# Gated linear attention: the last two out projections from seven block products, and a new place for VectorE's rank comparisons

## The chip, the cores and the metric

The kernel runs on one core of a Trainium2 chip. The metric is the device time of one execution in microseconds (us). Three executions of the kernel before the change took 910.1, 910.58 and 911.43 us; their median, 910.58 us, is the time that the changed kernel is compared with. All arithmetic is in float32; in the first feed-forward stage, alone, operands are split in two rounded parts.

## What is computed

The reference is a stack of four blocks on x of 2 x 1024 rows of 512 numbers, each followed by a layernorm. The change lies at the end of the third block and the beginning of the fourth. Cut to that:

```python
# third block: gated linear attention, o from a chunked scan
go = o @ Wog.T + x @ Wig.T
on = o * rsqrt(mean(o * o) + EPS) * g_norm_w
x  = layernorm(x + (on * (go * sigmoid(go))) @ Wo.T)
# fourth block: half of each batch's rows, by their score, go through a feed-forward
scores = x @ router_weight + router_bias
top, indices = top_k(scores, 512)                  # of 1024, for each batch
h = gelu(x[indices] @ w1 + b1)                     # 512 -> 2048
x[indices] += (h @ w2 + b2) * sigmoid(top)
x = layernorm(x)
```

## The kernel before, in words

The 2048 rows are worked on as four blocks of 512 rows, blk 0 to 3; batch 0 is blocks 0 and 1, batch 1 is blocks 2 and 3. Matrix products go to TensorE (PE), which writes to eight accumulation banks. They are picked from two rings of four, `mm_bank` and `acc_bank`; the fourth block alternates between the rings (`either_bank`, line 1528). VectorE (DVE) does the adds, the row statistics and the comparisons, ScalarE (ACT) the copies out of banks and the activations, GpSimd (POOL) a few sums, the powers and the gathers by index, and SyncE (SP) issues the other transfers.

Each engine runs its own queue in order. Where two queues meet, a semaphore makes one wait. The framework's scheduler sets each queue's order from the program, and `tc.issue_after(ins)` holds the instructions inside it back until `ins` has been placed: it is how the kernel's author moves work in a queue.

**Seven products for eight.** A product of matrices cut in 2 x 2 blocks needs eight block products. Most products of this kernel use seven, with sums of blocks made ahead on VectorE. In `finish_by_seven` (line 1375) the left factor is u (the gated rows, stored transposed in the tile uT), the right factor is W1o. `sums_of_W1o` (line 1358) makes four tiles T1 to T4 from W1o once; `sums_of_u` (line 1365) makes S1, S2 and A11 - A21 for each block of rows, three instructions. A product is four matmuls of 128 x 256, its result is added to x by two VectorE instructions (line 1393), and bank `grow` is added to by four products in turn, so that the next of them can only start once VectorE has read the last. `finish` (line 1410) does the same job with the plain sixteen matmuls of 128 x 512 and one add for each 128 rows (line 1423). Before the change blocks 0 and 1 use `finish_by_seven`, and blocks 2 and 3 use `finish`.

**The order around it.** The loop at line 1776 runs over blk. `attend(blk)` makes o of this block (tiles op, line 1257 and 1269), `gate(blk)` is a generator with the seven products of its gate (tiles go, line 864), between which the loop puts the out projection of block blk - 1. After it `scored_rows(blk - 1)` (line 1427) takes row statistics, the power on GpSimd, the layernorm and four scores. In blk 2, `route(0, ...)` ranks batch 0: eight transposes of the scores (tile rp, line 1458), then for each of eight columns two comparisons and one test for equals, each with a running sum (tiles cmp, lines 1467, 1470, 1473), then the ranks as an index (line 1480) and eight gathers on GpSimd (line 1483) that write the picked rows to HBM. `fetch(b)` (line 1506) reads them back and transposes them (tiles xs, xsTp).

**The fourth block.** `hidden(b, xs, h, beside)` (line 1532) computes h for one batch in four groups, g = 0 to 3, of seven products (tiles hp, line 1546); after each come VectorE's adds, lines 1558 to 1564 and 1571. Its sums of w1 are made by `sums_of_w1` (line 1848), its sums of x by `sums_of_x` (line 1516). The dictionary `beside` says what is placed between: `first_ranks` after the sixth product of group 0 holds the eight transposes of batch 1's scores and the first three columns of its ranking, the entry 0 has the sums of w1 for group 2 and then the other six steps of the ranking, and `next_rows`, after the sixth product of group 3, fetches batch 1's picked rows. `unpicked(blk)` (line 1498) normalizes a block once more and writes it to the output; block 0 is done in the loop's last round. Tiles of x, `x_room(i)`, and W1oT, the room of T1 to T4, are used again for sums of x, for h and for `kept`.

Of the kernel before, what the change touches and what calls it, by code (L numbers as in the profile page):

```python
# [21 lines left out]
P = 128  # L22
B, T, C = 2, 1024, 512
NB = 4
# [49 lines left out]
def body(ctx: ExitStack, tc: tile.TileContext, a: dict, out: bass.AP):  # L74
# [666 lines left out]
    class Gates:  # L741
# [10 lines left out]
            nc.scalar.copy(self.k4, lg[:, :, :, 32:])  # L752
            self.lq, self.lk = self.q4, self.k4

        def whole(self, lp):
            lg = lp.rearrange("p (i g d) -> p g i d", g=2, d=64)
            self.lq, self.lk = lg[:, :, :, :32], lg[:, :, :, 32:]
            self.k_exp()
            self.k_inverse()
            self.k_log()  # L760
            self.q_below()
            self.q_exp()
            self.q_share()
# [601 lines left out]
    def sums_of_u():  # L1365
# [6 lines left out]
        ins = nc.vector.tensor_sub(A21, A11, A21).ins  # L1372
        return (A11, A12, A21, A22), (S1, S2), ins

    def finish_by_seven(blk, u, w):

        (A11, A12, A21, A22), (S1, S2) = u
        (B11, B21, B22), (T1, T2, T3, T4) = w

        def product(ps, a, b, first, s, o):  # L1380

            with tc.issue_after(last_3[0]) if last_3[0] else contextlib.nullcontext():
                for r in range(2):
                    for m in range(2):
                        ins = nc.tensor.matmul(  # L1385
                            ps[:, 256 * r : 256 * r + 256], a[:, m, r * P : (r + 1) * P], b[:, m],
                            start=first and r == 0 and m == 0, stop=m == 1, skip_group_check=True,
                        ).ins
            last_3[0] = ins
            for r in range(2):  # L1390
                i = 2 * s + r
                x = x_t[blk][:, i, 256 * o : 256 * o + 256]
                nc.vector.scalar_tensor_tensor(
                    x, ps[:, 256 * r : 256 * r + 256], inv[blk][:, i : i + 1], x, ALU.mult, ALU.add
                )

        grow, p2, side = acc_bank("grow3"), mm_bank("P2"), mm_bank("P7")
        product(grow, A11, B11, True, 0, 0)
        product(p2, A12, B21, True, 0, 0)
        nc.vector.tensor_sub(A12, A12, S2)  # L1400
        yield
        product(grow, S2, T2, False, 1, 0)
        product(side, A21, T3, True, 1, 1)
        yield
        product(grow, S1, T1, False, 1, 1)
        product(side, A22, T4, False, 1, 0)
        product(grow, A12, B22, False, 0, 1)
        yield

    def finish(blk):  # L1410


        ao = [acc_bank("ao3") for _ in range(4)]
        steps = [(i, n) for i in range(4) for n in range(4)]
        if blk == NB - 1:
            steps = [(0, 0), (0, 1), (1, 0), (1, 1), (0, 2), (0, 3), (1, 2), (1, 3)] + steps[8:]
        for i, n in steps:
            k = (0, 2, 1, 3)[n]
            last_3[0] = nc.tensor.matmul(ao[i], uT[blk][:, k, i * P : (i + 1) * P], W1o[:, k], start=n == 0, stop=n == 3).ins  # L1419
        mv = sp.tile([P, 4, 2], F32, tag="mv", name="mv")  # L1420
        for i in range(4):
            x = x_t[blk][:, i]
            nc.vector.scalar_tensor_tensor(x, ao[i], inv[blk][:, i : i + 1], x, ALU.mult, ALU.add)
            row_stats(mv[:, i], x)
        return scored_rows(blk, mv)

    def scored_rows(blk, mv=None):

# [103 lines left out]
    def hidden(b, xs, h, beside):  # L1532

        (B11, B21, B22), (T1, T2, T3, T4) = xs

        def gelu(f):
            x = h[f // 4][:, f % 4]
            nc.scalar.activation(x, x, AF.Gelu_apprx_tanh, bias=b1[:, f : f + 1])

        def product(w, g, x):  # L1540

            ps = either_bank("hp")
            with tc.issue_after(last_hp[0]) if last_hp[0] else contextlib.nullcontext():
                for j in range(2):
                    for k in range(2):
                        ins = nc.tensor.matmul(  # L1546
                            ps[:, 256 * j : 256 * j + 256], pair_of(w, g)[:, k, j], x[:, k], start=k == 0, stop=k == 1
                        ).ins
            last_hp[0] = ins
            return ps.rearrange("p (j t) -> p j t", j=2)  # L1550

        for g in range(4):

            c = h[g].rearrange("p (j e) (s t) -> p j e s t", e=2, s=2)
            c11, c12, c21, c22 = (c[:, :, e, s] for e in range(2) for s in range(2))
            nc.scalar.copy(c11, product(wA11, g, B11))
            p2 = product(wA12, g, B21)
            nc.vector.tensor_add(c12, c11, product(wS2, g, T2))
            nc.vector.tensor_add(c11, c11, p2)
            nc.vector.tensor_add(c21, c12, product(wS3, g, T3))  # L1560
            p5 = product(wS1, g, T1)
            nc.vector.tensor_add(c22, c21, p5)
            nc.vector.tensor_add(c12, c12, p5)
            nc.vector.tensor_add(c12, c12, product(wS4, g, B22))
            if ("last", g) in beside:

                with tc.issue_after(last_hp[0]):
                    last_hp[0] = beside["last", g]()
            for j in range(2):
                gelu(4 * g + 2 * j)  # L1570
            ins = nc.vector.tensor_sub(c21, c21, product(wA22, g, T4)).ins
            for j in range(2):
                gelu(4 * g + 2 * j + 1)
            if g in beside:
                with tc.issue_after(ins):
                    beside[g]()
# [5 lines left out]
    def finish_ffn(w2, h):  # L1582
# [56 lines left out]
                add(ps, x, w, r)  # L1639
            return ps  # L1640

        kept = x_room(0, "kept")

        def steps(b):

# [128 lines left out]
    with tc.issue_after(scored):  # L1774
        next(ending)
    for blk in range(NB):
        if blk == 1 or blk == 2:
            *sums, summed = sums_of_u()
            if blk == 1:
                with tc.issue_after(summed):  # L1780
                    W1o_sums = sums_of_W1o()
        if blk == 2:
            new_front(3, gates)
        if blk == 1:
# [4 lines left out]
        if blk == 1:  # L1789
            with tc.issue_after(last_op[0]):  # L1790
                lp = turned_logits(lT)
            last_3[0] = last_turned[0]
            gates = Gates([wk.tile([P, 8, 32], F32, tag=n, name=n) for n in ("q3", "k3", "l3")])
            gates.whole(lp)
        if blk:
            o_sum(blk)
            gating = gate(blk)
            if blk < 3:
                finishing = finish_by_seven(blk - 1, sums, W1o_sums)
                for n in range(2):  # L1800
                    next(finishing)
                    next(gating)
                    if blk == 1 and n == 1:
                        with tc.issue_after(last_3[0]):
                            last_3[0] = gates.decayed(kd_room, jk.tile([P, 8, 32], F32, tag="junk", name="e3"))
                next(finishing)
                scored = scored_rows(blk - 1)
            else:
                scored = finish(blk - 1)
                for _ in range(2):  # L1810
                    next(gating)
        next(gating)
        if blk == 2:
            ranking = route(0, xT_tile("row"))
# [4 lines left out]
        if blk == 0:  # L1819
            o_sum(0)  # L1820
            nc.sync.dma_start(out=rw, in_=a["rw"].to_broadcast([P, C]))
            nc.sync.dma_start(out=b2, in_=a["b2"].to_broadcast([P, C]))
        other_sums(blk)
        if blk == 0:
            with tc.issue_after(scored_next):
                next(ending, None)
# [3 lines left out]
        for n, done in enumerate(gating):  # L1830
            if n == blk == 0:
                rms(0, sum2)
            if n == 2 and blk == 0:
                with tc.issue_after(last_3[0]):
                    last_3[0] = turn(3)
            if n == 1 and blk < 3:
                with tc.issue_after(done):
                    x_sum(blk + 1)
            if blk == 2:
                with tc.issue_after(done):  # L1840
                    for _ in range((3, 2, 2, 3)[n]):
                        next(ranking)
    wS1, wS2, wS4 = (spare[i][:, :, :512].rearrange("p (k h) (j f) -> p k h j f", h=2, f=P) for i in range(3))

    def pair_of(w, g):
# [10 lines left out]
                ins = nc.vector.tensor_tensor(pair_of(dst, g), pair_of(x, g), pair_of(y, g), op).ins  # L1856
        return ins

    sums_of_w1((0,))
    _, xs = fetch(0)  # L1860
    xs = sums_of_x(xs, W1oT)
    finish(3)
    sums_of_w1((1,))
    s3.close()
    wk = ctx.enter_context(tc.tile_pool(name="s4", bufs=2))
    h = [[*(wk.tile([P, 4, 512], F32, name=f"h0{g}", bufs=1) for g in range(3)), o_room]]
# [2 lines left out]
        nc.sync.dma_start(out=w2[g], in_=a["w2"][512 * g : 512 * (g + 1), :].rearrange("(f p) d -> p f d", p=P))  # L1869
    room = xT_tile("row")  # L1870
    ranking = route(1, room)

    def x_room(i, name):
        return xpool.tile([P, 4, ROW], F32, tag=f"x{i}", name=name)[:, :, :C]

    later = []

# [6 lines left out]
        return last_turned[0]  # L1884

    def next_sums():
        later[1] = sums_of_x(later[1], x_room(0, "xsums"))

    def first_ranks():
        rank_some(4)  # L1890
        return last_turned[0]

    hidden(0, xs, h[0], {("last", 0): first_ranks, ("last", 3): next_rows, 0: lambda: (sums_of_w1((2,)), rank_some(6)), 1: lambda: sums_of_w1((3,)), 3: next_sums})
    h.append([xT_tile("h10"), W1oT, later[0], x_room(1, "h13")])
    hidden(1, later[1], h[1], {g: lambda g=g: unpicked(g + 1) for g in range(3)})
    finish_ffn(w2, h)

# [51 lines left out]
```

## Time and profile before

| what | us |
|---|---|
| median of three executions | 910.58 |
| the profiled execution | 911.5 |
| its span, from its first instruction to its last | 909.7 |
| PE busy in the span | 891.9 |
| DVE busy in the span | 677.5 |
| ACT busy | 382.2 |
| POOL busy | 261.7 |

The profiled execution is 1.8 us longer than its span and 0.9 us above the median. PE is busy for 98% of the span, but a busy engine is only an average: in the stage of the change, between 640 and 760 us, PE still waits for others at some places. The granted clock of TensorE is 1.00 throughout that stage. A row of the timeline has the start and the length of a group of instructions on one engine, the line in the code, the operation, the tile written and the tile read, the shapes and a count; a matmul of float32 counts as two. In brackets stands how long the engine was idle before the group, and who released it.

### The profile page before, as it was taken

The page shows a single profiled execution, that of the slowest core. Times are in us where ns is not written, and L with a number is a line of the kernel's source. Part 1 is how long each engine was busy: PE and PEld are TensorE (multiplying, and loading weights), DVE is VectorE, ACT ScalarE, POOL GpSimd, SP SyncE. Part 2 cuts the span into 40 slices and gives each one's busy share as a digit, 9 for nine tenths or more (in the row PEclk, how much of TensorE's full clock was granted, in tenths as well). Part 3 has the DMA queues.
Part 4 walks back from the last instruction along what each step waited for, and adds up shares of the span by engine and source line. Part 5 has one row for each costly group of instructions (what it writes and reads, how often), then busy time and mean ns, then how long its engine had stood idle before and what let it go on. Part 6 is the DMA issues. An engine that isn't in the chain of part 4 may idle for free.

```text
span 909.7 us, 10988 instructions
## 1 busy us (share of the span) xinstructions
PE 891.9 (98%) x4037; PEld 698.8 (77%) x4037; DVE 677.5 (74%) x1304; ACT 382.2 (42%) x652; POOL 261.7 (29%) x229
## 2 busy tenths in 40 slices
PE   8999999999999999999999999999999999999996
PEld 5668786687688888888877677788676888888886
DVE  2569995589777787787769875857977976898535
ACT  2345343463467777877867534231201223120000
POOL 1120075200574357455654302020250030000112
PEclk9999999999999999999999999999999999999999
DMA  9632221200400000001001500000024220230001
GB/s 321 215 100 79 66 72 47 70 1 0 123 6 1 0 1 13 35 1 46 1 1 47 209 1 1 1 0 1 1 94 139 93 85 10 99 134 0 12 36 47
DMA packets 26135, 50.17 MB, mean 55 GB/s; under 512 B 4798, under 2 KB 5482, under 8 KB 25569
## 3 DMA queue, kind: packets, MB, share of 16 engines
q1 hardware_dynamic: 23441, 44.34, 14.5%
q0 software_dynamic: 1920, 4.22, 1.2%
q10 hardware_dynamic: 720, 0.92, 0.4%
q8 instruction: 32, 0.52, 0.3%
q14 instruction: 22, 0.18, 0.1%
HBM read 41.03 MB, written 10.54 MB: 57 GB/s over the span
## 4 chain that ended last, share of the span: by engine, by line
PE 81%; DVE 13%; ACT 2%; issue 2%; DMA 1%; POOL 0%; POOLq 0%; SPq 0%; DVEq 0%
PE yp L1632 10%; PE yp L896 9%; PE gatep L896 9%; PE hp L1546 9%; PE upp L896 9%; PE go L864 7%; PE xk L412 6%; PE grow L361 4%; PE P L361 3%; PE ao L559 2%; PE ao L1419 2%; PE grow L1385 1%; PE kp L585 1%; DVE cmp L1470 1%; PE op L1257 1%
## 5 line engine op out<-in xcount | busy, mean ns | idle before, releaser
L955 DVE TENSOR_TENSOR yp<-yp,ratio 128x512 f32<-128x512 f32 x160 | 103.3, 693 | 15.1 <-PE yp L896 15.0
L210 POOL TENSOR_TENSOR rs<-rs,table 128x4 f32<-128x4 f32 (+1 forms) x19 | 17.2, 904 | 293.8 <-DVE rs L209 293.6
L921 ACT ACTIVATE gatep<-gatep,scale 128x512 f32<-128x512 f32 x132 | 85.1, 656 | 34.9 <-PE gatep L896 32.2
L896 PE MATMUL yp<-wdn,hhi 128*128 128x512 f32 x176 | 71.7, 408 | 0.0
L896 PE MATMUL gatep<-x1Th,wgu 128*128 128x512 f32 x176 | 70.2, 399 | 0.0
L896 PE MATMUL yp<-wdn,hlo 128*128 128x512 f32 x176 | 69.8, 397 | 0.2 <-POOL hlo L930 0.2
L896 PE MATMUL gatep<-x1Tl,wgu 128*128 128x512 f32 x176 | 69.2, 393 | 0.3 <-DVE x1Tl L241 0.3
L896 PE MATMUL upp<-x1Tl,wgu 128*128 128x512 f32 x176 | 69.0, 392 | 0.0
L896 PE MATMUL upp<-x1Th,wgu 128*128 128x512 f32 x176 | 68.8, 391 | 0.0
L921 ACT ACTIVATE upp<-upp,scale 128x512 f32<-128x512 f32 x88 | 57.8, 662 | 11.1 <-PE upp L896 7.2
L930 POOL TENSOR_TENSOR hlo<-whole,hhi 128x512 fp32r<-128x512 f32 x43 | 55.6, 1292 | 3.5
L929 POOL CAST hhi<-whole 128x512 fp32r<-128x512 f32 x43 | 26.3, 612 | 99.8 <-DVE whole L927 89.6
L927 DVE SCALAR_TENSOR_TENSOR whole<-upp,scale,silu 128x512 f32<-128x512 f32 x43 | 32.3, 751 | 25.2 <-PE upp L896 19.0
L864 PE MATMUL go<-spare,spare 128*128 128x256 f32 x192 | 44.0, 381 | 0.0
L217 DVE BATCH_NORM_STATS2 st<-x 128x6 f32<-128x512 f32 x64 | 42.4, 679 | 0.4
L412 PE MATMUL xk<-pair,x 128*128 128x512 f32 x96 | 42.7, 592 | 0.0
L864 PEld LDWEIGHTS go<-spare,spare 128*128 128x128 f32 x192 | 36.0, 190 | 5.8 <-issue 1.2
L1279 POOL TENSOR_TENSOR sum<-sum,sq 128x512 f32<-128x512 f32 x12 | 18.2, 1520 | 77.1 <-issue 67.5
L896 PEld LDWEIGHTS gatep<-x1Th,wgu 128*128 128x128 f32 x176 | 33.1, 188 | 9.2 <-ACT gatep L921 1.3
L896 PEld LDWEIGHTS yp<-wdn,hhi 128*128 128x128 f32 x176 | 33.1, 188 | 8.8 <-DVE yp L955 1.1
L923 DVE TENSOR_SCALAR upp<-upp,scale 128x512 f32<-128x512 f32 x44 | 33.0, 753 | 9.1 <-PE upp L896 8.0
L896 PEld LDWEIGHTS gatep<-x1Tl,wgu 128*128 128x128 f32 x176 | 33.1, 188 | 8.0 <-DVE x1Tl L241 0.6
(468 smaller groups left out, 2109.5 us busy)
## 6 DMA issues: line engine op xcount, KB each, us to landing
pk<-in_gu SPq DMA_DIRECT2D x16, 352.0 KB, 3.6
x<-in_x SPq DMA_DIRECT2D x4, 1024.0 KB, 14.6
w<-in_w SPq DMA_DIRECT2D x1, 4096.0 KB, 12.3
xs<-picked SPq DMA_DIRECT2D x4, 1024.0 KB, 5.2
out<-x SPq DMA_DIRECT2D x4, 1024.0 KB, 4.2
w<-in_w SPq DMA_DIRECT2D x4, 1024.0 KB, 6.5
x0T<-in_xT SPq DMA_DIRECT2D x3, 1024.0 KB, 7.9
pk<-in_dn SPq DMA_DIRECT2D x11, 256.0 KB, 3.2
```

The source lines that it names most:

```text
L217: nc.vector.bn_stats(st, x)
L361: ins = nc.tensor.matmul(ps[:, 256 * r : 256 * r + 256], a[:, k, r * P : (r + 1) * P], b[:, k], start=first and r == 0 and k == 0, stop=k ...
L412: ins = nc.tensor.matmul(acc_of[b][c], x_t[blk][:, i, c * P : (c + 1) * P], pairs_of["k", blk][i // 2][:, i % 2], start=blk % 2 == 0 and i ...
L864: ins = nc.tensor.matmul(ps[:, 256 * m : 256 * m + 256], w[:, k, m], b[:, k, 256 * half : 256 * half + 256], start=first and m == 0 and k ...
L896: nc.tensor.matmul(ps, w, x, start=start and n == 0, stop=stop and n == 1, skip_group_check=True)
L921: nc.scalar.activation(ps, ps, AF.Copy, scale=s)
L923: nc.vector.tensor_scalar(ps, ps, s, None, ALU.mult)
L927: nc.vector.scalar_tensor_tensor(self.whole, ps, s, self.silu, ALU.mult, ALU.mult)
L930: nc.gpsimd.tensor_sub(lo, self.whole, hi.bitcast(F32))
L955: nc.vector.tensor_tensor(self.y[:, i] if g == NI - 1 else ps, ps, ratio[:, g], ALU.mult)
L1546: ins = nc.tensor.matmul(ps[:, 256 * j : 256 * j + 256], pair_of(w, g)[:, k, j], x[:, k], start=k == 0, stop=k == 1).ins
L1632: nc.tensor.matmul(ps[:, 256 * r : 256 * r + 256], x(r, j), w(j), start=j == 0, stop=j == NJ - 1)
```

## The change

1. Blocks 2 and 3 use `finish_by_seven` too, and `finish` is gone. `sums_of_u` runs in each round, and once more after the loop.
2. In round 1, the gates' later steps (`rest`) are placed after the adds of the first product (`first_add`); in each round `other_sums` are placed after those of the third (`second_add`).
3. The ranking of batch 0 had its ten steps all in round 2, as 3, 2, 2, 3 between the gate's parts. It has 1, 3, 1, 0 there, two after round 3's sums of u and three after `first_add`.
4. The sums of w1 for groups 0 and 1 are placed after the add of the last gate's fifth product (`gate_sums_end`).
5. In `hidden(0, ...)` the last six steps of batch 1's ranking are placed one at a time between the adds of group 1 and no longer ahead of them.
6. Rooms: the sums of x for batch 0 go into the room of block 0's x, which `unpicked(0)` writes out, as W1oT is still in use; those of batch 1 into W1oT.

```diff
-        def whole(self, lp):
+        def begin(self, lp):
             ...
             self.k_exp()
+
+        def rest(self):
             self.k_inverse()
...
+                ins_of[0] = nc.vector.scalar_tensor_tensor(
                     x, ps[:, 256 * r : 256 * r + 256], inv[blk][:, i : i + 1], x, ALU.mult, ALU.add
+                ).ins
+            return ins_of[0]
...
+        first_add[blk] = product(grow, A11, B11, True, 0, 0)
...
+        second_add[blk] = product(grow, S2, T2, False, 1, 0)
...
+            def add(*x):
+                nonlocal added
+                added += 1
+                ins = nc.vector.tensor_add(*x).ins
+                if (g, added) in beside:
+                    with tc.issue_after(ins):
+                        beside[g, added]()
...
-        kept = x_room(0, "kept")
+        kept = W1oT
...
-        if blk == 1 or blk == 2:
+        if blk:
             *sums, summed = sums_of_u()
-            if blk == 1:
-                with tc.issue_after(summed):
+            with tc.issue_after(summed):
+                if blk == 1:
                     W1o_sums = sums_of_W1o()
+                if blk == 3:
+                    for _ in range(2):
+                        next(ranking)
...
+            finishing = finish_by_seven(blk - 1, sums, W1o_sums)
+            for n in range(2):
                 next(finishing)
+                if blk == 1 and n == 0:
+                    with tc.issue_after(first_add[0]):
+                        gates.rest()
+                if blk == 3 and n == 0:
+                    with tc.issue_after(first_add[2]):
+                        for _ in range(3):
+                            next(ranking)
+                next(gating)
...
-        other_sums(blk)
+        with tc.issue_after(second_add[blk - 1]) if blk else contextlib.nullcontext():
+            other_sums(blk)
...
-                    for _ in range((3, 2, 2, 3)[n]):
+                    for _ in range((1, 3, 1, 0)[n]):
                         next(ranking)
+            if blk == 3 and n == 1:
+                gate_sums_end = done
...
-    sums_of_w1((0,))
+    with tc.issue_after(gate_sums_end):
+        sums_of_w1((0,))
+    *sums, _ = sums_of_u()
     _, xs = fetch(0)
-    xs = sums_of_x(xs, W1oT)
-    finish(3)
-    sums_of_w1((1,))
+    xs = sums_of_x(xs, x_room(0, "xsums0"))
+    for _ in finish_by_seven(3, sums, W1o_sums):
+        pass
+    scored_rows(3)
+    with tc.issue_after(gate_sums_end):
+        sums_of_w1((1,))
...
-    hidden(0, xs, h[0], {("last", 0): first_ranks, ("last", 3): next_rows, 0: lambda: (sums_of_w1((2,)), rank_some(6)), 1: lambda: sums_of_w1((3,)), 3: next_sums})
-    h.append([xT_tile("h10"), W1oT, later[0], x_room(1, "h13")])
+    one_rank = lambda: rank_some(1)
+    hidden(0, xs, h[0], {
+        ("last", 0): first_ranks, ("last", 3): next_rows, 0: lambda: (sums_of_w1((2,)), one_rank()), 1: lambda: sums_of_w1((3,)),
+        (1, 2): one_rank, (1, 3): one_rank, (1, 5): one_rank, (1, 6): lambda: rank_some(2), 3: next_sums,
+    })
+    h.append([xT_tile("h10"), x_room(0, "h11"), later[0], x_room(1, "h13")])
```

More of the change, by code (lines that the diff above doesn't have):

```diff
@@ L1373, in sums_of_u @@
         return (A11, A12, A21, A22), (S1, S2), ins
+    first_add, second_add = {}, {}
     def finish_by_seven(blk, u, w):
@@ L1392, in product @@
                 x = x_t[blk][:, i, 256 * o : 256 * o + 256]
-                nc.vector.scalar_tensor_tensor(
+                ins_of[0] = nc.vector.scalar_tensor_tensor(
                     x, ps[:, 256 * r : 256 * r + 256], inv[blk][:, i : i + 1], x, ALU.mult, ALU.add
-                )
+                ).ins
+            return ins_of[0]
+        ins_of = [None]
         grow, p2, side = acc_bank("grow3"), mm_bank("P2"), mm_bank("P7")
-        product(grow, A11, B11, True, 0, 0)
+        first_add[blk] = product(grow, A11, B11, True, 0, 0)
         product(p2, A12, B21, True, 0, 0)
@@ L1401, in finish_by_seven @@
         yield
-        product(grow, S2, T2, False, 1, 0)
+        second_add[blk] = product(grow, S2, T2, False, 1, 0)
         product(side, A21, T3, True, 1, 1)
@@ L1408, in finish_by_seven @@
         yield
[L1410 to L1425, printed above, removed]
     def scored_rows(blk, mv=None):
@@ L1556, in hidden @@
             nc.scalar.copy(c11, product(wA11, g, B11))
+            added = 0
+            def add(*x):
[5 more added lines that the diff above has]
+                        beside[g, added]()
             p2 = product(wA12, g, B21)
-            nc.vector.tensor_add(c12, c11, product(wS2, g, T2))
-            nc.vector.tensor_add(c11, c11, p2)
-            nc.vector.tensor_add(c21, c12, product(wS3, g, T3))
+            add(c12, c11, product(wS2, g, T2))
+            add(c11, c11, p2)
+            add(c21, c12, product(wS3, g, T3))
             p5 = product(wS1, g, T1)
-            nc.vector.tensor_add(c22, c21, p5)
-            nc.vector.tensor_add(c12, c12, p5)
-            nc.vector.tensor_add(c12, c12, product(wS4, g, B22))
+            add(c22, c21, p5)
+            add(c12, c12, p5)
+            add(c12, c12, product(wS4, g, B22))
             if ("last", g) in beside:
@@ L1793, in body @@
             gates = Gates([wk.tile([P, 8, 32], F32, tag=n, name=n) for n in ("q3", "k3", "l3")])
-            gates.whole(lp)
+            gates.begin(lp)
         if blk:
@@ L1797, in body @@
             gating = gate(blk)
[L1798 to L1805, printed above, removed]
-                next(finishing)
[L1807 to L1811, printed above, removed]
+            finishing = finish_by_seven(blk - 1, sums, W1o_sums)
+            for n in range(2):
+                next(finishing)
+                if blk == 1 and n == 0:
[6 more added lines that the diff above has]
+                next(gating)
+                if blk == 1 and n == 1:
+                    with tc.issue_after(last_3[0]):
+                        last_3[0] = gates.decayed(kd_room, jk.tile([P, 8, 32], F32, tag="junk", name="e3"))
+            next(finishing)
+            scored = scored_rows(blk - 1)
         next(gating)
@@ L1857, in sums_of_w1, with x_room @@
         return ins
-    sums_of_w1((0,))
-    _, xs = fetch(0)
-    xs = sums_of_x(xs, W1oT)
-    finish(3)
-    sums_of_w1((1,))
+    def x_room(i, name):
+        return xpool.tile([P, 4, ROW], F32, tag=f"x{i}", name=name)[:, :, :C]
+    with tc.issue_after(gate_sums_end):
+        sums_of_w1((0,))
+    *sums, _ = sums_of_u()
+    _, xs = fetch(0)
+    xs = sums_of_x(xs, x_room(0, "xsums0"))
[4 more added lines that the diff above has]
+        sums_of_w1((1,))
     s3.close()
@@ L1871, in body @@
     ranking = route(1, room)
-    def x_room(i, name):
-        return xpool.tile([P, 4, ROW], F32, tag=f"x{i}", name=name)[:, :, :C]
     later = []
@@ L1886, in next_sums @@
     def next_sums():
-        later[1] = sums_of_x(later[1], x_room(0, "xsums"))
+        later[1] = sums_of_x(later[1], W1oT)
     def first_ranks():
```

## The prediction, made before the changed kernel had run

> **What bounds the kernel now.** I read the page's busy shares first, then PE's waits from 470 us on, then PE's and DVE's timelines between 636 and 760 us, and busy time by stretches.
>
> ```profile
> PE 891.9 (98%) x4037; PEld 698.8 (77%) x4037; DVE 677.5 (74%) x1304; ACT 382.2 (42%) x652; POOL 261.7 (29%) x229
> ```
>
> Its waits from 470 us on (after the names: idle us, how often, the longest):
>
> ```profile
> PE go L864 <- DVE uT L1337: 1.4, 2, 1.2
> PE grow L1385 <- DVE x L1393: 1.1, 1, 1.1
> PE hp L1546 <- DVE index L1480: 0.7, 1, 0.7
> ```
>
> PE sets the end, and from 470 us on it waits four times, 3.2 us in all, each time for DVE. But DVE is close behind:
>
> ```profile
> 640.00:674.00 34.00, 33.79 (x134) 22.75 (x135) 29.05 (x66) 7.76 (x13) 15.10 (x13) 1.00 0.10 33
> 674.00:716.00 42.00, 41.76 (x172) 30.58 (x171) 33.18 (x72) 5.40 (x9) 3.40 (x3) 1.00 0.44 150
> 716.00:754.00 38.00, 37.28 (x177) 32.57 (x176) 31.44 (x79) 11.78 (x18) 8.04 (x8) 1.00 0.18 56
> ```
>
> After the length stand PE, PEld, DVE, ACT, POOL: in the 114 us of the change DVE works 93.7, and much of the rest is idle time in which it waits for a result (the 5.2 us for ao). So work added to DVE has little room, and its place in the queue matters. Four places of PE's timeline carry the prediction:
>
> ```profile
> 650.33 13.90 PE L1419 MATMUL ao<-W1o,uT 128*128 128x512 f32 x32
> ...
> 691.38 13.90 PE L1419 MATMUL ao<-W1o,uT 128*128 128x512 f32 x32
> ...
> 715.48 1.04 PE L1458 MATMUL rp<-table,score 128*128 128x128 f32 x8
> ...
> 753.57 1.91 PE L226 MATMUL xsTp<-table,xs 128*128 128x128 f32 x16
> ```
>
> From here on "ao", "rp" (batch 1's score transposes) and "xsTp" (its picked rows) are these. rp needs the finished scores, xsTp the gathered rows.
>
> **What goes.** Costs are start to start, so that a pipeline's restart is in them.
> - Two plain projections: the next groups start 13.73 us after each (650.33 to 664.06, 691.38 to 705.12). Seven products are 28 matmuls of 128x256 at 1.73 us for four (604.39 - 602.66): 12.08. Gain 1.65 twice, 3.3.
> - Round 1's wait: a product starts at 558.81, while the one ahead ends by 557.52 (554.07 + 3.45), and it takes 1.83 for 1.73. Its adds now stand ahead of the gates' steps, right behind o's sum, and are done at 554.1. Gain 1.39. The gates' results (l, q) come by 561, needed at 564.5 and 571.6: covered.
> - Round 2's wait: go ends at 638.45, two op matmuls cover 0.44, the next go starts at 640.21 and takes 3.56 for 3.45. The add it waits for now stands ahead of the comparisons, done by 635.8 on the old clock. Gain 1.42.
> - The last gate's wait: 685.68 to 686.08 and its restart, 0.5. The add now stands ahead of w1's sums.
> - Group 2's wait at 734.51 for the adds behind the whole ranking: 0.97 with restart. Between the ranking's steps, the adds come at least 4 us before PE needs their banks.
>
> Sum: 7.6 us, if nothing else became late.
>
> **What comes.** DVE gets, for each of the two blocks, 14 adds at 0.40 (0.79 for two, 620.13 to 620.92) and four block sums at 0.60, in place of four adds at 0.65: 5.3 us more. No page or trace of before shows it in its new place, so I walk the built program's queues with before's durations, on the changed kernel's clock (all 1.39 earlier from round 1 on).
>
> *Block 2's projection.* PE: go to 640.5, op 7.0, two products, go: the third product could start at 654.4. It adds to the bank of the first, so it waits for that one's two adds. DVE: c22's add 633.8; two steps of scan and gate sums to 636.3; three columns of ranking 4.7; c12's add, ACT's silu, two gated products (1.33) to 644.15; a column (1.60), two gated products, three sums of u to 649.1; two columns to 652.7; then o's sum. That took 1.13 us alone (654.94) but 1.91 and 1.98 beside POOL's sums of squares (551.38, 601.87). With 1.9 and 0.79 for the adds: 655.4. New wait 0.95; with 1.13 it is 0.2. I take the longer, since POOL's sums fall in the same stretch. [...]
>
> The projection then ends (E2) at 667.5. POOL's gathers of batch 0, index at 660.2, eight at 1.28, are through by 670.8, before the power needs POOL (E2 + 3.8).
>
> *From E2 to block 3's first adds, DVE sets the time.* The layernorm starts at E2 + 5.83 (as 619.93 to 625.76): 673.3. From there DVE is never idle for long: layernorm 1.83, scores 2.45, block 0's statistics 2.5, two gate adds 1.3, the power's round trip 1.66 (680.05 to 681.71), layernorm 1.83, c12's add 0.6, two w1 sums 1.2, gated products 1.33, w1 0.6, gated products 1.33: 689.9. Now w1's next sum, three sums of u and four of x, 4.9, and the first adds 0.79: 695.7. PE has its last gate product by 685.5, transposes by 687.25, waits 0.7 for the gated products, has two products by 691.3, and fills 2.59 with six hp matmuls: ready at 693.85, it waits 1.85 for those adds. Five more products: E = 704.4 (ao ended at 705.12). Among these sums, the first of x also waits for block 0's output transfer, as it takes that room: issued at 684.9, landing 4.2 later (that row of before) is 689.1, needed at 691.1: hidden, 2 us to spare.
>
> *rp.* Before, 24 hp matmuls (10.36 us) stood between the last ao and rp, and DVE needed 8.3 (705.12 to the scores' bias add at 713.22, whose end is 713.45). Now six of the 24 are already spent, so PE is ready at E + 7.8. DVE needs longer: all four tiles' statistics come after the last product, and three hidden adds stand ahead of the scores. Adds 0.79, statistics 2.6, hidden adds 1.3, power 1.35, layernorm 1.83 with one add 0.6 under the power, scores 2.45, an add 0.6, the bias: E + 11.3. New wait 3.5, rp at 715.7, against 715.48. All the gain so far is gone.
>
> *xsTp.* Before: rp to index 18.96 us (715.48 to 734.44), index to landed rows 17.4 (the transfer issued at 746.55 took 5.3), that is 1.7 before xsTp. Now seven hidden adds, some w1 sums, stand between the ranking's steps: comparisons start at rp + 1.74 as before, then 20.8 us of queue, index at rp + 22.6, rows at rp + 40.0. PE comes at rp + 37.1 (21 products and rp itself). New wait 2.9; xsTp at 755.7, against 753.57.
>
> After that PE's order and durations are as before, without a wait. **Sum**: +2.1 us, of which 7.6 are gains and some 9.8 new waits. The profiled execution would take 911.5 + 2.2 = 913.7 with a span of 911.9; the median, 0.9 lower, **912.8 us**.
>
> The moved rooms, the sums placed behind `second_add` and the changed order of ACT's copies cost nothing: their readers come 5 us later or more; without that cover each costs at most its length, 1.2.
>
> **Rivals.**
> - *PE stays the bound* (0.11): DVE's chain is shorter than I count, so that rp and xsTp find their data. For it: 5.2 us of before's DVE idle time lie at the ao waits, which go. Against: rp's wait follows from one queue, E to score, without any guess. It decides where scores are ready by E + 7.8. Then the 7.6 us stay but for small waits: 903 to 908, say 905.
> - *Only the rp wait* (0.31): the index comes 2 us earlier or the rows land faster, and PE's waits at block 3's adds are shorter: 909.9 (rp + 0.2, less 0.97), from 908.8 to 912.4. This is no change that can be told: about 0.2%, 1.8 us, is what a measurement of this kernel can tell.
> [...]
> - *The forecast* (0.44): 911.5 to 914.6; a fifth of it counts as no change.
>
> That the change doesn't do what it says is excluded by the built order: both ao groups are gone.
>
> **Numbers.** Faster by over 0.2% 0.11 (the first rival), within 0.40 (the second, and a fifth of the forecast), slower by over 0.2% 0.49. The range leaves out the best case and the far end: 908.6 to 915.6.
>
> **What would show it.** PE's waits of 558.81, 640.21, 686.08 and 734.51 gone; grow's third product of block 3 waiting about 1.9 for x's adds; rp idle 3 to 4 us released by DVE's score line; xsTp idle 2 to 3 released by the transfer of picked rows; index 22 to 23 us after rp. If rp does not wait, or xsTp finds its rows, the forecast is wrong by that term.

## The result and the profile after

| | before | after |
|---|---|---|
| median of six executions each, us | 910.65 | 915.62 (914.72 to 916.11) |
| ratio, 95% interval | | 1.005 [1.004, 1.006] |
| the profiled execution, us | 911.5 | 915.6 |
| its span, us | 909.7 | 913.8 |

The changed kernel is slower by 5.0 us: the forecast's side, but more than twice its 2.2 us, and at the upper end of its range. It lies above the forecast's own stretch (911.5 to 914.6). The page's busy line of the changed kernel:

```profile
PE 891.9 (98%) x4085; PEld 709.8 (78%) x4085; DVE 684.0 (75%) x1332; ACT 382.2 (42%) x652; POOL 260.1 (28%) x229
```

PE is as busy as before, although seven products save it 3.3 us. 1.7 us of this is slow time, which this line cannot show; the clock below does. Another 1.8 us lies in the first 20.4 us, ahead of the change: there PE is busy for 19.4 us and was for 17.5 before, with 1.84 us of waiting for a load in its place. DVE has 6.5 us more. PE's waits of the changed kernel from 470 us on (idle us in all, how often, the longest):

```profile
PE rp L1448 <- DVE score L1431: 3.4, 1, 3.4
PE grow L1389 <- DVE x L1397: 2.2, 2, 1.5
PE xsTp L226 <- DMA xs<-picked: 2.1, 1, 2.1
PE go L866 <- DVE uT L1339: 1.0, 1, 1.0
PE grow L1389 <- DVE uT L1317: 0.5, 1, 0.5
```

Three of before's four waits are gone; that of the last gate, which should have gone too, has grown from 0.24 to 1.0, and 8.2 us of others have come, all forecast with their place and releaser. Where they stand, from PE's timeline of the changed kernel:

```profile
654.26 1.99 PE L1389 MATMUL grow<-spare,uS 128*128 128x256 f32 x8 [0.72 <-DVE x L1397]
...
666.46 0.95 PE L1287 MATMUL mp<-table,sum 128*128 128x1 f32 x8
...
682.37 3.72 PE L866 MATMUL go<-spare,Wog 128*128 128x256 f32 x16 [1.05 <-DVE uT L1339]
...
688.34 2.23 PE L1389 MATMUL grow<-W1o,uT 128*128 128x256 f32 x8 [0.50 <-DVE uT L1317]
...
696.53 1.99 PE L1389 MATMUL grow<-spare,uS 128*128 128x256 f32 x8 [1.45 <-DVE x L1397]
...
716.60 1.97 PE L1448 MATMUL rp<-table,score 128*128 128x128 f32 x8 [3.39 <-DVE score L1431]
718.36 2.67 PE L1536 MATMUL hp<-xsums,w 128*128 128x256 f32 x8
...
757.65 1.94 PE L226 MATMUL xsTp<-table,xs 128*128 128x128 f32 x16 [2.08 <-DMA xs<-picked]
```

This execution runs 1.05 us ahead of the profiled one of before from the start, as a load for which PE waited until 8.25 us in the kernel before happened to land in time here; from 20 us to 550 us the distance is constant. With that 1.05 added, every stretch can be set beside the forecast (start to start, changed less before):

| stretch | forecast | measured |
|---|---|---|
| round 1's wait | -1.39 | -1.39 |
| round 2's wait | -1.42 | -1.41 |
| block 2's projection (to mp, the small matmuls behind it) | -0.70 | -0.66 |
| mp to the first product of block 3 | +0.04 | +1.47 |
| from there to rp | +3.65 | +4.16 |
| rp to xsTp | +1.91 | +2.96 |
| sum | +2.1 | +5.1 |

After xsTp both kernels run alike. Three stretches are longer than forecast, by 1.4, 0.5 and 1.05.

**The first of them** is on GpSimd. Its timeline in the changed kernel:

```profile
660.42 2.28 POOL L1473 DMA_INDIRECT picked<-x,index  x1 [0.75 <-DVE index L1470]
663.01 1.36 POOL L1473 DMA_INDIRECT picked<-x,index  x1 [0.31 <-issue]
664.67 0.97 POOL L1473 DMA_INDIRECT picked<-x,index  x1 [0.30 <-issue]
...
671.07 0.97 POOL L1473 DMA_INDIRECT picked<-x,index  x1 [0.30 <-issue]
672.04 1.07 POOL L1290 TENSOR_TENSOR ms<-ms,table 128x4 f32<-128x4 f32 x1
673.07 1.02 POOL L210 TENSOR_TENSOR rs<-rs,table 128x4 f32<-128x4 f32 x1
```

The two powers of block 2 start at once behind the eighth gather: they had been waiting in the queue. DVE had sent the input of the first at 670.1, and then stood still:

```profile
674.12 1.92 DVE L212 TENSOR_SCALAR x<-x,mv,rs 128x512 f32<-128x512 f32 x4 [3.66 <-POOL rs L210]
```

The two powers themselves take 2.1 us (672.04 to 674.1). Without the gathers they could have started at 670.2, 1.8 earlier.

**The third** is partly PE's clock. Busy time by stretches of the changed kernel (length, then PE, PEld, DVE, ACT, POOL, then the granted clock):

```profile
715.00:716.50 1.50, 0.00 (x0) 0.00 (x0) 1.50 (x7) 0.00 (x0) 0.00 (x0) 1.00 0.00 0
716.50:717.00 0.50, 0.40 (x2) 0.40 (x3) 0.50 (x2) 0.00 (x0) 0.00 (x0) 0.53 0.00 0
717.00:718.00 1.00, 1.00 (x7) 1.00 (x6) 0.82 (x2) 0.25 (x1) 0.00 (x0) 0.50 0.00 0
718.00:719.00 1.00, 1.00 (x5) 0.91 (x4) 0.00 (x0) 0.73 (x2) 0.00 (x0) 0.50 0.00 0
719.00:720.00 1.00, 1.00 (x3) 0.80 (x3) 0.78 (x1) 0.98 (x2) 0.00 (x0) 0.53 0.00 0
720.00:721.00 1.00, 1.00 (x6) 0.89 (x5) 1.00 (x7) 0.99 (x2) 0.00 (x0) 1.00 0.00 0
```

After 3.39 us without work PE ran at half its clock here, 0.50 for 3.4 us. The eight transposes of rp take 1.76 us (716.60 to 718.36) where they took 0.87 before, the next product 2.51 for 1.73: 1.67 us of PE's time, all of it counted as busy. The last section has a wait as long behind which the clock stayed at 1.00. The prediction forecast an idle time of 3.5 us and did not price this.

### The profile page after: what moved, and what is told of

Its sections match the earlier page's. It is cut to its first block, busy times and chain, and to the rows that moved or that the text cites. A ratio compares the mean times of both kernels' runs of the same rounds, so it can differ in the third digit from the quotient of the medians.

```text
span 913.8 us, 11110 instructions
## 1 busy us (share of the span) xinstructions
PE 891.9 (98%) x4085; PEld 709.8 (78%) x4085; DVE 684.0 (75%) x1332; ACT 382.2 (42%) x652; POOL 260.1 (28%) x229
## 4 chain that ended last, share of the span: by engine, by line
PE 77%; DVE 9%; issue 9%; POOL 2%; ACT 2%; DMA 1%; POOLq 0%; DVEq 0%; ACTq 0%
PE yp L1632 10%; PE yp L898 9%; PE gatep L898 9%; PE upp L898 9%; PE go L866 7%; PE xk L412 6%; PE hp L1536 5%; PE grow L361 4%; PE P L361 3%; PE kp L585 2%; PE grow L1389 2%; PE ao L559 2%; POOL picked L1473 1%; PE op L1259 1%; PE P L1389 1%
```

## The experiments

My theory was a **chain**: block 3's last adds, statistics, power, scores, rp, ranks, index, gathers, fetch. It runs over DVE, GpSimd and the transfers, and sets when xsTp can start; PE's own savings ahead of it are worth only what they bring that chain forward. The rivals were **DVE's work** (6.5 us more of it cost the same in any order) and **PE's work** (whatever shortens PE, its clock too, shortens the time). Each run was timed five rounds or more beside the kernel before on the same chip; so the ratio is what compares them, and the changed kernel's is 1.0055.

| run | us (before beside it) | ratio, 95% interval |
|---|---|---|
| rank_ahead | 914.53 (911.29) | 1.0035 [1.0021, 1.0048] |
| block3_plain | 912.60 (911.29) | 1.0013 [1.0004, 1.0022] |
| both_plain_ahead | 915.20 (911.29) | 1.0043 [1.0029, 1.0057] |
| warm_wait | 918.55 (911.29) | 1.0080 [1.0066, 1.0094] |
| gathers_split | 914.43 (910.80) | 1.0038 [1.0025, 1.0052] |
| block3_plain_ahead | 908.51 (910.80) | 0.9976 [0.9966, 0.9985] |
| split_block3_plain_ahead | 907.02 (910.80) | 0.9959 [0.9945, 0.9972] |
| clock_kept | 916.95 (910.80) | 1.0066 [1.0052, 1.0080] |
| both_plain_early | 908.14 (911.26) | 0.9964 [0.9952, 0.9976] |
| split_ahead | 911.61 (911.26) | 1.0008 [0.9999, 1.0017] |
| seven_repaired | 911.65 (911.26) | 1.0008 [0.9999, 1.0017] |

**rank_ahead**

```diff
-        ("last", 0): first_ranks, ("last", 3): next_rows, 0: lambda: (sums_of_w1((2,)), one_rank()), 1: lambda: sums_of_w1((3,)),
-        (1, 2): one_rank, (1, 3): one_rank, (1, 5): one_rank, (1, 6): lambda: rank_some(2), 3: next_sums,
+        ("last", 0): first_ranks, ("last", 3): next_rows, 0: lambda: (sums_of_w1((2,)), rank_some(6)), 1: lambda: sums_of_w1((3,)),
+        3: next_sums,
```

> Undoes one part of the change: batch 1's ranking stands again wholly ahead of group 1's hidden adds, all else as in the changed kernel (915.62 us). Chain theory: xsTp is set by a chain on DVE, GpSimd and the transfers (last x adds, statistics, scores, transposes, ranks, index, gathers, fetch). The index comes some 3.5 us earlier (about 19.9 us after rp instead of 23.4), the 2.2 us wait for the picked rows goes, and the bunched adds cost at most 0.5: 913.4 us (913.2 to 914). Rival, DVE's work in all: the same instructions in another order cost the same, the wait only moves to the hidden products' banks: 915.6 us, within 0.5.

xsTp no longer waits, and stands 38.86 us behind rp (717.74 to 756.60) instead of 41.05: 2.2 less, as the chain theory said. In the ratios it is 0.0020, 1.8 us, with an interval that overlaps the changed kernel's, so the times alone do not show it; the same edit on a plain block 3, below, does.

**block3_plain** puts back the plain `finish` for block 3 alone.

```diff
-    *sums, _ = sums_of_u()
     _, xs = fetch(0)
     xs = sums_of_x(xs, x_room(0, "xsums0"))
-    for _ in finish_by_seven(3, sums, W1o_sums):
-        pass
-    scored_rows(3)
+    finish(3)
```

> Only block 2 by seven products; block 3 is projected by the plain sixteen matmuls, all else as in the changed kernel. Chain theory: what counts in block 3 is the time from its first product to the scores. Plain: 13.7 us after the start its last product is through, each tile's statistics are done beside it, and 10.4 us of hidden products cover the 8.3 us to the scores, so rp starts at about 712.4 on this clock instead of 716.6 and the index, at the same distance, takes xsTp 5 us forward: 910.5 us (909.9 to 911.2), although PE has 1.7 us more to do. Rival, PE's work: the plain block costs its 1.7 us: 917.2 us. Rival, DVE's load: half of the 5.3 us of added work goes: 913 us.

PE's timeline of this run:

```profile
688.84 14.00 PE L1425 MATMUL ao<-W1o,uT 128*128 128x512 f32 x32 [0.49 <-DVE uT L1317]
...
713.04 1.04 PE L1467 MATMUL rp<-table,score 128*128 128x128 f32 x8
...
753.05 2.56 PE L226 MATMUL xsTp<-table,xs 128*128 128x128 f32 x16 [2.71 <-DMA xs<-picked]
755.41 2.99 PE L1555 MATMUL hp<-xsums,w 128*128 128x256 f32 x8
```

rp comes 24.2 us after the block's first product instead of 28.3, without a wait, and xsTp 5.1 us earlier (753.05 against 757.65, in an execution that is 0.5 late from the start), although PE has more to do: the chain theory, against PE's work. Against DVE's work this run is no witness: DVE is busy for 679.3 us here and for 684.0 in the changed kernel, 4.7 less, so that rival would give nearly the same gain (the expectation took half of 5.3, which by its terms is what one block adds). The gain is 3.8 us by the ratios and not the 5.1 of the expectation, since now the wait at xsTp was followed by half the clock (0.50 in 755 to 757): the first product behind it starts at 755.41 and the next at 758.23, where 753.05 + 1.73 and 1.73 more would be 756.5. It did not fall every time: three of the eleven executions have a mean granted clock of 0.998 and took 911.3 to 911.4 us, the other eight 0.996 and 911.9 to 913.6. Their medians are 1.3 us apart, which is what the fall goes with in this kernel.

**both_plain_ahead** has the edits of rank_ahead and block3_plain, and also puts back `finish` for block 2, with batch 0's last three ranking steps behind its first add.

```diff
+            else:
+                scored = finish(2)
+                with tc.issue_after(first_add[2]):
+                    for _ in range(3):
+                        next(ranking)
```

> Only the moves, without the seven products: both blocks plain, batch 1's ranking ahead of the adds as in the kernel before; the adds ahead of rank comparisons and of w1's sums, the gates' later steps, batch 0's ranking and the rooms as in the changed kernel. Chain theory: the waits at 558.81 (1.39) and 640.21 (1.42) go, that of the last gate (0.5) may go, and nothing else becomes late: 910.65 less 2.8 to 3.3, so 907.3 to 907.9 us. Rival, the moves themselves bring new waits (batch 0's ranking ends later, block 0's output is a room that sums wait for): 910 us or more.

A miss of 7 us, and the run that told most. PE had one long wait (another is 0.7, at a bank behind batch 1's ranking):

```profile
687.28 6.14 PE L866 MATMUL go<-spare,Wog 128*128 128x256 f32 x16 [4.30 <-DVE uT L1339]
```

and GpSimd's timeline says why:

```profile
673.43 1.23 POOL L1492 DMA_INDIRECT picked<-x,index  x1 [0.18 <-issue]
...
682.64 0.97 POOL L1492 DMA_INDIRECT picked<-x,index  x1 [0.30 <-issue]
683.63 1.06 POOL L210 TENSOR_TENSOR rs<-rs,table 128x4 f32<-128x4 f32 x1
```

My own edit let the index slip behind block 2's scores, so that the next power, that of block 0's layernorm, stood behind eight gathers; DVE's layernorm waited 7.85 us for it, and an add for the gate stood behind the layernorm. The same queue stands in the changed kernel, with the 1.8 us shown above.

**gathers_split**

```diff
             apart(ins.ins, rows)
+            if b == 0 and i == 5:
+                yield
...
             scored = scored_rows(blk - 1)
+            if blk == 3:
+                with tc.issue_after(last_power[0]):
+                    next(ranking)
```

> The changed kernel, with batch 0's eight gathers cut in two on GpSimd's queue: six stand ahead of block 2's powers as now, two behind them. Nothing else moves. Queue theory: in the changed kernel the layernorm of block 2 waits 3.7 us for a power that stands behind the gathers (their end at 672.04; the power could start at 670.1). With two gathers behind it the layernorm starts at 672.2 instead of 674.1, and the whole chain on DVE up to block 3's scores, ranks and picked rows comes 1.9 earlier, with PE behind it: 913.8 us (913.4 to 914.3) where the changed kernel takes 915.62. Rival, DVE's work: the wait is absorbed by what DVE has still to do, 915.6 us, within 0.5.

```profile
668.69 0.97 POOL L1475 DMA_INDIRECT picked<-x,index  x1 [0.30 <-issue]
670.45 1.04 POOL L1290 TENSOR_TENSOR ms<-ms,table 128x4 f32<-128x4 f32 x1 [0.78 <-DVE mv L218]
671.48 1.00 POOL L210 TENSOR_TENSOR rs<-rs,table 128x4 f32<-128x4 f32 x1
672.66 1.04 POOL L1475 DMA_INDIRECT picked<-x,index  x1 [0.19 <-issue]
```

In GpSimd's timeline of this run the power now waits for its input and not for the gathers. PE's waits of 1.05 and 0.50 at the last gate and the first product are gone, and rp starts at 715.09, 1.5 earlier (1.7, since this execution is some 0.2 late from the start). By the ratios it is 1.5 us, with intervals that overlap. The clock differs from the changed kernel's in this trace: it stayed at 1.00 after rp's wait of 3.39, and fell to 0.50 (755 to 758) at xsTp's of 2.71. So this pair is not free of the clock; the traces of the next two runs are.

**block3_plain_ahead** joins rank_ahead and block3_plain, **split_block3_plain_ahead** also gathers_split.

> Block 3 plain and batch 1's ranking ahead of the adds, block 2 by seven. With block 3 plain alone PE waited 2.7 us for the picked rows and ran the next 3.4 us at half its clock (1.7 us more). Chain theory: the index comes 3.5 us earlier, so both go, and the wait for a bank behind the ranking (0.97) comes back: 912.6 less 2.7, less 1.7, plus 1.0: 909.2 us (908.5 to 910). Rival, only the wait goes and the clock's fall is chance: 910.9 us. Rival, DVE's work in all: 912.6.

> The two last edits together: block 3 plain, batch 1's ranking ahead of the adds, and two of batch 0's gathers behind block 2's powers; block 2 by seven. If the queue on GpSimd and the chain to the picked rows are the two causes, they add up: 909.2 less 1.9, 907.3 us (906.6 to 908.3), under the kernel before. If GpSimd's queue costs nothing once the chain is short: 909.2.

Both came out as expected. They differ in gathers_split's edit alone and their traces have no fall of the clock in this stage: 908.51 us (908.02 to 909.12) against 907.02 (906.47 to 907.23) on the same chip, 1.5 us for the queue on GpSimd. PE's waits from 540 us on in the second:

```profile
PE grow L1389 <- DVE x L1397: 0.7, 1, 0.7
PE hp L1559 <- DVE index L1491: 0.7, 1, 0.7
```

With block 3 plain, the ranking's place is worth 0.0037 (3.4 us, the clock's fall included), without any overlap of the intervals: DVE's work is the same in both, so that rival is out. The second is faster than both kernels: 0.9959 [0.9945, 0.9972].

**warm_wait and clock_kept** put matmuls of constants into PE's idle time: 24 ahead of rp; then ten there and six ahead of xsTp.

```diff
+            if b == 1 and h == 0:
+                for _ in range(10):
+                    last_hp[0] = nc.tensor.matmul(rp[:, :P], ident, ident, start=True, stop=True).ins
...
```

> The changed kernel with 24 matmuls of constants (some 2.6 us of work, into the bank that the transposes overwrite) in PE's idle time ahead of rp. It tells what the clock costs that falls to 0.50 after that idle time (716.5 to 720). Chain theory: the clock stays at 1.00, the transposes take 0.87 instead of 1.76 us, the index and the picked rows come 0.9 earlier, and the other 0.8 us of PE's gain is spent waiting for the rows: 914.7 us (914.3 to 915.1). Rival, PE's work sets the end: the whole 1.67 us comes back: 913.9 us. If the clock falls all the same: 915.6.

> The changed kernel with ten matmuls of constants ahead of rp and six ahead of the second xsTp, inside PE's two idle times (2.2 and 1.3 us of work, by 0.223 for one as the 24 of the earlier run took 5.36). The clock should stay at 1.00 through both. Chain theory: only the transposes' 0.9 us are on the chain to the picked rows, the rest of what PE gains is spent waiting: 914.7 us (914.3 to 915.2). Rival, PE's work sets the end: the whole 1.67 us comes back, 913.9 us. If the clock does not matter: 915.6.

Both missed. In warm_wait I had taken a matmul for one record of 0.11 us; each is two, the 24 took 5.36 (713.18 to 718.54), and rp came late. In clock_kept the clock stayed at 1.00 through rp, and the index was ready 22.7 us after rp began (716.83 to 739.51) instead of 23.5 (716.60 to 740.11): the 0.8 that slow transposes cost the chain. But there the last gather, begun at 749.04, let the fetch go only at 753.10, 4.06 later, where the changed kernel and all other runs show 2.6; an instruction fetch of about 20 KB ran on the transfer engines at 750 to 751, among the gathers' last packets. Whether it was the cause was not tried. Then the clock fell after xsTp's 2.89 us of waiting. So the 0.8 is shown in the trace, and these two runs give no time for the clock as a whole; the 1.3 us between the executions of block3_plain are the nearest to one.

**both_plain_early** is both_plain_ahead with batch 0's ranking wholly in round 2, behind the adds.

```diff
-                    for _ in range((1, 3, 1, 0)[n]):
+                    for _ in range((1, 3, 1, 5)[n]):
```

> Only the moves, without the seven products, as in the run both_plain_ahead, but with batch 0's last five ranking steps still in round 2, so that its index and the eight gathers come ahead of block 2's powers by as much as in the kernel before. Queue theory: the 4.3 us wait of both_plain_ahead (a layernorm 7.9 us behind a power that stood behind the gathers) goes, and the moves are worth what was forecast of them, 1.39 and 1.42, and perhaps the 0.5 of the last gate: 910.7 less 2.8, 907.9 us (907.3 to 908.4). Rival, the moves bring other waits: 910 or more.

PE's only wait from 540 us on:

```profile
PE hp L1555 <- DVE index L1489: 0.7, 1, 0.7
```

908.14, ratio 0.9964: the moves alone are worth 3.3 us, what was forecast of them (1.39 + 1.42 + 0.5). The queue on GpSimd, with the clock's fall behind the wait, explains both_plain_ahead's loss: from one profiled execution to the other the last gate starts 4.5 us later and the transposes behind it 7.0 (0.24 of shift between the two taken off). both_plain_early is level with split_block3_plain_ahead (0.9959), which also differs in the place of batch 0's ranking, so seven products in block 2 gain nothing that these runs can tell.

**split_ahead and seven_repaired** keep seven products in both blocks and have the edits of gathers_split and rank_ahead; the second also puts rp, and with it the whole ranking, behind the first product of group 1, where PE need not wait. Its edit beside split_ahead:

```diff
+            if ("first", g) in beside:
+                with tc.issue_after(last_hp[0]):
+                    last_hp[0] = beside["first", g]()
...
-        rank_some(4)
+        rank_some(10)
...
-        ("last", 0): first_ranks, ("last", 3): next_rows, 0: lambda: (sums_of_w1((2,)), rank_some(6)), 1: lambda: sums_of_w1((3,)),
+        ("first", 1): first_ranks, ("last", 3): next_rows, 0: lambda: sums_of_w1((2,)), 1: lambda: sums_of_w1((3,)),
```

> Both blocks by seven products; two of the gathers behind block 2's powers, and batch 1's ranking ahead of the adds. Chain theory: with the gathers cut alone (914.43) PE waited 2.7 us for the picked rows and then had half its clock (1.4 us); both go, the wait for a bank behind the ranking (up to 1.0) may come back: 910.8 us (910.1 to 911.6). What is left over 907.02, where only block 3 is plain, is what seven products cost in block 3: its adds, the 3.4 us wait of rp and what the clock does after it. Rival, PE's work: 1.7 us less than 907.02, so 905.4.

> As split_ahead, with rp and the whole ranking placed after the first product of group 1, so that 3.5 us more of hidden products stand ahead of rp and PE does not wait there. Chain theory: the scores are ready no earlier (714.6 on the changed kernel's clock), and six hidden adds and four sums of w1 now stand ahead of the comparisons; index 734.5, rows 751.9, PE ready for them at 748.3: the wait moves from rp to xsTp. 909.9 us, 911.4 if the clock falls after that wait. Rival, PE's work sets the end once rp does not wait: 905.4 us.

split_ahead and split_block3_plain_ahead differ only in block 3: 1.0008 against 0.9959, 4.5 us for seven products there, which save PE 1.65. In seven_repaired PE's waits from 470 us on are these:

```profile
PE xsTp L226 <- DMA xs<-picked: 2.8, 1, 2.8
PE grow L1389 <- DVE x L1397: 2.2, 2, 1.5
PE hp L1540 <- DVE h L1559: 1.1, 1, 1.1
```

rp's 3.4 us are gone and 2.8 at xsTp and 1.1 at a bank have come, for the same time within 0.1 us. PE's work as the bound would have given 905.4. The chain theory's own figure, 909.9 with the clock kept, was too low as well: on the changed kernel's clock the index came at 735.2 for 734.5 and the rows at 753.0 for 751.9. This is the chain theory's clearest run: PE's wait moves along the chain, and its end stays.

## Why the prediction was right, and where it fell short

- **What goes.** Right: 1.39, 1.42 and the bank behind the ranking went as worked out. The 0.5 of the last gate did not go in the changed kernel, but did where GpSimd's queue was free (both_plain_early).
- **Block 2's projection.** Right, 0.95 against 0.99, by two errors that cancel. o's sum took 1.14 and not 1.9: it began at 652.21, between GpSimd's sums (650.86 to 652.13, the next at 653.12). A comparison (L1463) that began at 651.35, inside the first of these, took 0.93 for the usual 0.35, and held o's sum back. In the kernel before, one that began at 653.82, inside the sum of 653.39 to 654.65, took 0.99.
- **"POOL's gathers of batch 0 ... are through by 670.8, before the power needs POOL."** This step failed. On the prediction's clock the first gather began 1.3 after the index's forecast time, the first two took 4.25 for 2 x 1.28, and the last ended at 673.1. The power came 1.8 late, DVE's layernorm with it, and 1.4 of it reached block 3's first product; gathers_split gives 1.5 us back, and so does the same edit on a plain block 3.
- **"From E2 to block 3's first adds, DVE sets the time."** Right, with 1.85 forecast and 1.72 measured at the third product. The first two products took 3.99 for 3.46, the 0.5 of the second stretch. The trace shows where: inside them PE's weight loads stood idle for 0.37 us (until 689.00) and 0.30 (until 690.93), released by DVE's gated products (L1317). The prediction let PE wait for these once, ahead of the two.
- **rp.** Right: 3.5 forecast, 3.55 measured, with rp at E + 11.3 as forecast (E, the end of block 3's projection, is 705.27 here). What it sets off was left out: half the clock for 3.4 us, 0.8 of it on the chain.
- **xsTp.** The mechanism was right. The index took 23.5 for 22.6, which is the clock's 0.8 and 0.1; the rows took 17.5 for 17.4.
- **"All the gain so far is gone."** Right in substance: the change's moves were worth 3.3 us, and block 3's seven products, with its ranking and the gathers, took back more. The rival with PE as the bound is refuted by seven_repaired.
- **The range.** That it held, by its far end, is in part luck. Block 0's output landed 5.3 us after its issue at 685.83, where 4.2 was forecast, but still ahead of the first sum of x at 692.00, and what the comparison lost beside GpSimd is in the 0.99 above: neither made the time longer than forecast. Of the 3.0 us by which the stretches above exceed the forecast, 1.4 came with the gathers' queue, 0.5 with the gated products and 0.9 with the clock, none of which is in its sum.

## What to carry to other kernels

When an engine that is 98% busy is given less to do, find the next point at which it must have another's result, and follow the chain back from there: what shortens the engine's own work ahead of that point turns into a wait. When a step is moved, look at what it issues on a third engine: eight gathers of 1.28 us ahead of a small power cost 1.5 us here, and more where they slipped further. A forecast idle time of about three microseconds on PE should be priced with the clock behind it: here the clock fell to 0.50 behind six of the ten waits of 2.6 to 4.3 us, and in the changed kernel this took 1.67 us of PE's time.

## What was not expected of the hardware

The clock's fall is not decided by the length of the idle time alone. After 3.39 or 3.40 us ahead of rp it fell to 0.50 in the changed kernel and in rank_ahead, and stayed at 1.00 in gathers_split and split_ahead. After waits of 2.6 to 2.9 us ahead of xsTp it fell in block3_plain (2.71), gathers_split (2.71) and clock_kept (2.89), and stayed in warm_wait (2.60) and seven_repaired (2.82). After 2.08 us, at the changed kernel's xsTp, it stayed. In both_plain_ahead it fell at a wait of 4.30. By the mean clock of the stretches around them, the falls of five of these executions lasted 3.4 us each; that of both_plain_ahead lasted 5.2 us or more (0.50 from 687 on, 0.95 as the mean of 692 to 694). A fall began before PE started again (by 0.6 us at gathers_split's xsTp) or after (by 1.4 in clock_kept); in the 3.4 us ahead of those five PE had stood idle for 2.0 (clock_kept) to 3.3 us (the changed kernel). Most kernels with such waits also spread more from one execution to the next: 911.0 to 913.7 for split_ahead, 915.1 to 918.7 for clock_kept, against 906.5 to 907.2 for split_block3_plain_ahead, which has none; gathers_split, with two of them, did not (913.8 to 914.5).
